# Splitting the causal convolution of sequence 1 over three engines in a fused Mamba and transformer kernel

## The chip, the cores and the metric

The kernel runs on one core of one Trainium2 chip, in one launch. The metric is device time in microseconds (us) of that core. Three runs of the kernel before gave 946.91, 949.45 and 950.11 us; their median is 949.45 us. A core has five engines that matter here: TensorE (PE, matrix products), VectorE (DVE), ScalarE (ACT), GpSimd (POOL) and SyncE (SP, which only issues DMAs). Each works through its own queue in order, and they wait for one another through semaphores. SBUF is the working memory, with 128 partitions; PSUM is the smaller memory into which TensorE writes its products, cut into banks.

## The reference

Four blocks with residuals and layer norms, on two sequences of 512 tokens with 512 features each. Only the first block matters here, a Mamba layer with 1024 channels, 16 states per channel and a causal convolution of four taps:

```python
proj = hidden_states @ W_in.T
x, gate = (proj[..., :D_IN], proj[..., D_IN:])
xpad = jnp.pad(x, ((0, 0), (K - 1, 0), (0, 0)))
xc = conv_b
for j in range(K):                               # K = 4
    xc = xc + conv_w[:, j] * xpad[:, j:j + L, :]
x = jax.nn.silu(xc)
...
state = state * dA + (dt_t * u_t)[..., None] * B_t[:, None, :]   # along time
y = jnp.einsum('bdn,bn->bd', state, C_t)
```

After it come a gated FFN with 4-bit weights ("gptq"), a small attention and a mixture block.

## The kernel before, in words

**Layout.** Channels lie on the partitions, in 8 blocks of 128 (index c), and the 512 time steps along the free dimension. A tile is 128x512 float32. The two sequences are handled one after the other (b = 0, 1).

**The scan loop.** The heart of the first block is the loop at L1152: 128 steps s, for b, then c, then gi (8 pairs of states). Step s handles a 128x1024 tile: DVE multiplies `du` by B (`times_B`, L1092; one step ahead, so step s computes the product for s+1), DVE runs the recurrence (`scan`, L1096), POOL multiplies by C (`times_C`, L1102), and TensorE adds the tile into `y` with an identity matrix (`sums`, L1124; two steps behind). ACT writes the decay factors exp(dt A) into one of two PSUM tiles (`exps`, L1076); those for step s+2 can be written only when scan s has read its tile. Every eighth step also has a `du` product (L1090) and a product of the gate with `y` (`fin`, L1130).

**What is planned beside it.** All other work of the neighbourhood is woven into these steps by a planner written in Python. A counter of ticks runs at two per step: the odd tick 2s+1 comes ahead of `times_B(s+1)`, the even tick 2s+2 between `times_B(s+1)` and `scan(s)`; `exps(s+2)` and `times_C(s)` come after the scan. A job is a generator that gives out some instructions and yields the number of ticks until it goes on. Jobs run in the order in which they were spawned. Extra work on POOL asks `pool_turn` (L181) for a turn, and there is one turn per step; who finds it taken tries again at the next tick. TensorE's extra products come from one generator, `stream` (L1030), in a fixed order; each step has a budget of 3.5 us (`STEP`), a product counts 0.86 us (`MM`), and `until` (L797) holds the stream back until a named job is done. `pin` (L407) fixes the order of tracing on PE, ACT, DVE and POOL, so the planner's order is the order of the queues. SP is not pinned.

**The jobs that share the steps 18 to 42.** They are

- `proj_x` and `x_job` (L787, L772): for each block c of sequence 1, four products into a PSUM bank `px`; then ACT evicts the bank with the newest tap and the bias into `u1_c` (`evict_x`, L478); two ticks later DVE adds the three older taps, each one an instruction that reads `px` and `u1_c` (`conv`, L485); two ticks later ACT makes a sigmoid (two instructions, L780 and L781); two ticks later, with a turn, POOL multiplies it in (L784). The convolutions lie in the steps 19, 22, 24, 27, 30, 32, 34 and 38, on even ticks: after `times_B(s+1)` and ahead of `scan(s)` on DVE's queue.
- the words of the 4-bit weights (`GateUpWords.steps`, L276): a new one every three steps; DVE takes out a nibble (L235), ACT converts it (L293), POOL subtracts and multiplies (L297, L301, a turn each), SP stores it. `stream` waits for the last word ("words") before it goes on to the gates of sequence 1.
- `gate` (L759) and `gate_job`: four products, three ACT instructions, one POOL product with a turn.
- `ranks1` and `rows1` (L862, L873): small products from all eight `u1_c`, after the last of these (`until(("u1", 7), 3)`); their result feeds the B and C tiles of sequence 1, which `states` (L553) loads in the steps 56 to 63. Then `fc1_expert` (L952) and `out_tiles` (L978), the latter from step 66 on, when `fin` of block 7 of sequence 0 is out.

Scratch rows come from small pools: `jrow` (tag "j", three buffers) and `trow` (tag "t", two buffers, for the sigmoids). The framework sets all semaphores from the accesses that it records. `ranks_out` (L542) is one more place that the prediction uses: there ACT (L544) and, for sequence 0, DVE (L548) copy two different parts of one PSUM tile `pt` to two different SBUF tiles.

Of the kernel before, what the change touches and what calls it, by code (L numbers as in the profile page):

```python
# [12 lines left out]
AF = mybir.ActivationFunctionType  # L13
# [7 lines left out]
S = 512  # L21
# [7 lines left out]
NCH = D_IN // P  # L29
# [4 lines left out]
KCONV = 4  # L34
# [22 lines left out]
def tile_sandwich(  # L57
# [5 lines left out]
    nc = tc.nc  # L63
# [34 lines left out]
    ch = const.tile([P, NCH, NCP], F32, name="ch")  # L98
# [82 lines left out]
    def pool_turn():  # L181

        while pool_at[0] == (now[0] - 1) // 2:
            yield 1
        pool_at[0] = (now[0] - 1) // 2
# [242 lines left out]
    with ExitStack() as mamba:  # L428
# [9 lines left out]
        def new_u(name):  # L438
            return up_.tile([P, S], F32, tag="u", name=name)
# [4 lines left out]
        def jrow(name):  # L444
            return jp.tile([P, S], F32, tag="j", name=name)

        def trow(name):
            return jp.tile([P, S], F32, tag="t", name=name, bufs=2)
# [7 lines left out]
        for b in range(B):  # L456
            t_ = smp.tile([R_DT + 1, S], F32, tag=f"dtT{b}", name=f"dtT{b}")
# [19 lines left out]
        def evict_x(c, ps, uc):  # L477
            nc.scalar.activation(  # L478
                uc, ps, AF.Identity,
                bias=ch[:, c, KCONV : KCONV + 1], scale=ch[:, c, KCONV - 1 : KCONV],  # L480
            )

        def conv(c, ps, uc):
            for s in range(1, KCONV):
                nc.vector.scalar_tensor_tensor(  # L485
                    uc[:, s:], ps[:, : S - s], ch[:, c, KCONV - 1 - s : KCONV - s],
                    uc[:, s:], ALU.mult, ALU.add,
                )
# [90 lines left out]
        with ExitStack() as p1:  # L579
# [5 lines left out]
            def bank1(i, name):  # L585
                return mbank(name) if i % 2 else ps_1.tile([P, S], F32, tag="mm", name=name)
# [28 lines left out]
            for c in range(NCH):  # L615
                w = w_in(0, 0, c)
                ps = bank1(c, f"px0_{c}")
                for k in range(KH):
                    nc.tensor.matmul(
                        ps, w[:, k, ts(c % 2, P)], xT[0][:, k, :], start=(k == 0), stop=(k == KH - 1)  # L620
                    )
                    if k == 1 and c >= 2:
                        for i in range(TB):
                            ranks_of(0, c - 2, i, pr)
                uc = u[0][c] = new_u(f"u0_{c}")
                evict_x(c, ps, uc)
                early = [gw.steps() for _ in range(4 if c == 0 else 0)]
                for word in early:
                    next(word)
                for word in early[:2]:  # L630
                    next(word)
                conv(c, ps, uc)
                nc.scalar.activation(uc, uc, AF.Silu)
                for word in early:
                    for _ in word:
                        pass
                if c:
                    gw.word()
                for _ in range((0, 0, 2, 0, 1, 0, 1, 0)[c]):
                    gw.word(nc.gpsimd)  # L640
# [42 lines left out]
        with ExitStack() as p2:  # L683
# [51 lines left out]
            def release(name):  # L735
                next(t for t in turns if t[0] == name)[1] = now[0]
# [35 lines left out]
            def x_job(c, ps):  # L772
                uc = u[1][c] = new_u(f"u1_{c}")
                evict_x(c, ps, uc)
                yield 2
                conv(c, ps, uc)
                release(f"px1_{c}")
                yield 2
                th = trow(f"tu1_{c}")
                nc.scalar.activation(th, uc, AF.Tanh, scale=0.5)  # L780
                nc.scalar.activation(th, th, AF.Identity, bias=half[:, 0:1], scale=0.5)  # L781
                yield 2
                yield from pool_turn()
                nc.gpsimd.tensor_mul(uc, th, uc)  # L784
                st["u1", c] = now[0]

            def proj_x(c):  # L787
                w = w_in(0, 1, c)
                if c + 2 - c % 2 < NCH:
                    w_in(0, 1, c + 2 - c % 2)  # L790
                while now[0] < 2 * (NGI * (c - 3) + 4):
                    yield None
                ps = yield from bank(f"px1_{c}")
                yield from in_proj(1, ps, w, c % 2)
                spawn(x_job(c, ps), 2)
# [402 lines left out]
        with ExitStack() as p3:  # L1198
# [9 lines left out]
            for j in range(NCH // 2):  # L1208
                w = wo_pair(1, 0, j)
                for e in range(2):  # L1210
                    c = 2 * j + e
# [305 lines left out]
```

## Time and profile before

| | |
|---|---|
| median of three runs | 949.45 us |
| the profiled execution | 943.15 us, its span 941.0 us |
| mean granted TensorE clock | 0.966 |
| busy: PE / DVE / ACT / POOL | 91% / 71% / 46% / 52% of the span |
| scan loop (first to last `times_C`) | 73.8 to 567.1 us |
| convolutions of sequence 1 | 141.0 to 226.1 us |

The profile is one execution recorded by the hardware. Its page has busy times by engine, a picture of the span in 40 slices, the chain of work that ended last, and groups of instructions by line. The trace behind it answers with timelines of one engine (start in us, duration in us, engine, line, operation, output<-inputs, shape, and in brackets the idle time ahead of it and who ended it), with waits, and with busy times in chosen windows. Consecutive instructions on an engine overlap by some hundredths of a microsecond, so three of 0.75 us in a row take 2.23 us. All times in the following are of this execution.

### The profile page before, as it was taken

What the parts mean: (1) busy time and instruction counts of PE and PEld (TensorE: products, weight loads), DVE (VectorE), ACT (ScalarE), POOL (GpSimd) and SP (SyncE); (2) the same over time, 40 slices, a digit from 0 to 9 for tenths busy, and PEclk for the clock granted to TensorE, in tenths of its full rate; (3) what the DMA queues carried; (4) which work ended last, traced back from release to release, by engine and by line L of the source; (5) the groups of instructions that cost most, each with busy time, mean ns of one, the idle gap of its engine ahead of it and who ended that gap; (6) DMA issues with size and microseconds to landing.
All of it is one profiled execution on the core that took longest, in us unless ns stands there. A gap on an engine that the chain in (4) does not pass through costs nothing.

```text
span 941.0 us, 7171 instructions
## 1 busy us (share of the span) xinstructions
PE 860.5 (91%) x2188; PEld 385.9 (41%) x2188; DVE 669.7 (71%) x770; ACT 428.3 (46%) x654; POOL 486.1 (52%) x356
## 2 busy tenths in 40 slices
PE   6989979879999898699999989899999998999994
PEld 3434433323544343244444434344544444445441
DVE  5778999999999998999999995525600034535235
ACT  3368875665667645656666530215320014322122
POOL 7758887767887777777788884520000000011012
PEclk9989999989999999799999999999999999999998
DMA  6549100110004954101110022356223121200101
GB/s 196 207 136 373 37 35 31 38 38 23 23 25 158 300 161 157 40 1 45 45 45 24 16 68 101 128 143 201 59 64 90 59 90 45 67 12 24 55 0 45
DMA packets 43816, 80.08 MB, mean 85 GB/s; under 512 B 7774, under 2 KB 20937, under 8 KB 43778
## 3 DMA queue, kind: packets, MB, share of 16 engines
q1 hardware_dynamic: 41506, 73.64, 24.0%
q0 software_dynamic: 1984, 5.47, 1.6%
q10 hardware_dynamic: 288, 0.52, 0.2%
q8 instruction: 17, 0.28, 0.1%
q14 instruction: 21, 0.17, 0.1%
HBM read 68.37 MB, written 11.24 MB: 85 GB/s over the span
## 4 chain that ended last, share of the span: by engine, by line
PE 40%; DVE 29%; issue 12%; DMA 5%; POOL 5%; ACT 3%; SPq 1%; DVEq 0%; POOLq 0%; ACTq 0%
DVE bx L1096 11%; DVE bx L1092 8%; PE pd L1445 6%; PE py L1124 5%; PE pup L1382 5%; PE fg L373 4%; PE fu L373 4%; PE fo L1298 3%; DMA B<-scr 2%; PE po L990 2%; DVE u L485 2%; PE fo L1235 2%; PE pr L1413 1%; POOL bx L1102 1%; PE pg L749 1%
## 5 line engine op out<-in xcount | busy, mean ns | idle before, releaser
L1102 POOL TENSOR_TENSOR bx<-bx,C 128x1024 f32<-128x1024 f32 x128 | 302.2, 2362 | 105.0 <-DVE bx L1096 77.9
L1096 DVE TENSOR_TENSOR_SCAN bx<-da,bx 128x1024 f32<-128x1024 f32 x128 | 291.7, 2279 | 0.3 <-ACT da L1076 0.2
L1124 PE MATMUL py<-bx,ident 128*128 128x512 f32 x480 | 234.5, 619 | 25.4 <-POOL bx L1102 21.8
L1076 ACT ACTIVATE da<-dt,A 128x511 f32<-128x511 f32 x256 | 176.5, 691 | 141.4 <-DVE bx L1096 136.8
L1092 DVE TENSOR_TENSOR bx<-du,B 128x1024 f32<-128x1024 f32 x127 | 152.9, 1205 | 3.8 <-POOL bx L1104 1.2
L1124 PEld LDWEIGHTS py<-bx,ident 128*128 128x128 f32 x480 | 91.9, 197 | 150.2 <-issue 97.3
L387 POOL TENSOR_TENSOR sd<-ve,half 128x4 f16<-128x4 f16 x2 | 2.1, 1042 | 113.1 <-DVE ve L385 113.1
L1311 DVE TENSOR_TENSOR it<-it,fu 128x512 f32<-128x512 f32 (+1 forms) x11 | 7.6, 687 | 73.6 <-PE fu L373 73.6
L749 PE MATMUL pg<-xT,w_g 128*128 128x512 f32 x114 | 56.3, 624 | 0.7 <-ACT dt L573 0.7
L1382 PE MATMUL pup<-hT_l,wup 128*128 128x512 f32 x128 | 56.2, 593 | 0.0
L1445 PE MATMUL pd<-wdn,hid 128*128 128x512 f32 x128 | 55.3, 593 | 0.0
L129 POOL TENSOR_TENSOR rs_lo<-ve_lo,mhalf 128x1 f32<-128x1 f32 x8 | 5.4, 680 | 76.7 <-DVE ve_lo L127 76.7
L1235 PE MATMUL fo<-wd,it 128*128 128x512 f32 (+1 forms) x88 | 40.0, 616 | 3.6 <-DMA wd<-wd_d 3.6
L1021 PE MATMUL fg<-hT_f,wg 128*128 128x512 f32 (+1 forms) x88 | 42.5, 594 | 0.0
L373 PE MATMUL fg<-hT_f,wg 128*128 128x512 f32 (+1 forms) x88 | 41.9, 615 | 0.7 <-ACT hT_f L173 0.7
L485 DVE SCALAR_TENSOR_TENSOR u<-px,ch,u 128x511 f32<-128x511 f32 (+2 forms) x48 | 35.9, 747 | 8.3 <-ACT u L478 7.1
L1021 PE MATMUL fu<-hT_f,wu 128*128 128x512 f32 (+1 forms) x88 | 40.4, 594 | 1.4 <-ACT dt L573 1.4
L373 PE MATMUL fu<-hT_f,wu 128*128 128x512 f32 (+1 forms) x88 | 39.8, 593 | 0.0
L1298 PE MATMUL fo<-wd,it 128*128 128x512 f32 (+1 forms) x88 | 39.6, 592 | 0.0
L1445 PEld LDWEIGHTS pd<-wdn,hid 128*128 128x128 f32 x128 | 24.2, 190 | 30.7 <-issue 30.1
L1310 ACT ACTIVATE it<-fg 128x512 f32<-128x512 f32 (+1 forms) x11 | 6.6, 597 | 65.7 <-PE fg L373 65.7
L1382 PEld LDWEIGHTS pup<-hT_l,wup 128*128 128x128 f32 x128 | 23.9, 190 | 28.2 <-issue 28.2
(243 smaller groups left out, 1168.2 us busy)
## 6 DMA issues: line engine op xcount, KB each, us to landing
wo<-in_W_outT SPq DMA_DIRECT2D x20, 512.0 KB
B<-scr SPq DMA_DIRECT2D x16, 512.0 KB
C<-scr SPq DMA_DIRECT2D x16, 512.0 KB
wg<-wgu_d SPq DMA_DIRECT2D x10, 512.0 KB
wu<-wgu_d SPq DMA_DIRECT2D x10, 512.0 KB
w_x<-in_W_in SPq DMA_DIRECT2D x8, 512.0 KB
wgu_d<-w_gu POOLq DMA_DIRECT2D x16, 256.0 KB, 2.4
w_g<-in_W_in SPq DMA_DIRECT2D x8, 512.0 KB
```

The source lines that it names most:

```text
L373: nc.tensor.matmul(ps[:m], w[:, kc, e * P : e * P + m], hT[:, kc, :], start=(kc == 0), stop=(kc == KH - 1),)
L749: nc.tensor.matmul(ps, w[:, k, ts(e, P)], xT[b][:, k, :], start=(k == 0), stop=(k == KH - 1))
L1021: nc.tensor.matmul(ps[:m], wt[j][a][:, kc, e * P : e * P + m], hT[:, kc, :], start=(kc == 0), stop=(kc == KH - 1),)
L1076: nc.scalar.activation(das[s % 2][:, i, 1:], st["dt", b, c][:, 1:], AF.Exp, scale=A[:, c, n : n + 1])
L1092: nc.vector.tensor_mul(bx, st["du"].unsqueeze(1).to_broadcast([P, NG, S]), Bbs[b][gi])
L1096: nc.vector.tensor_tensor_scan(flat, das[s % 2].rearrange("p n t -> p (n t)"), flat, 0.0, ALU.mult, ALU.add)
L1102: nc.gpsimd.tensor_mul(bxs[s], bxs[s], Cbs[b][s % NGI])
L1124: nc.tensor.matmul(st["y"], ident, bx[:, i, :], start=False, stop=last)
L1235: nc.tensor.matmul(fo[t], its[i][:m, ts(t, P)], w[:m, e], start=(i == 0), stop=(i == len(IC) - 1),)
L1298: nc.tensor.matmul(fo[t], its[i][:m, ts(t, P)], w[:m], start=(i == 0), stop=(i == len(IC) - 1),)
L1382: nc.tensor.matmul(ps, w[:, kc, ts(e, P)], src[kc], start=(kc == 0), stop=(kc == KH - 1))
L1445: nc.tensor.matmul(pd, hid[kc][:, ts(i, P)], wdn[kc], start=(kc == 0), stop=(kc == INT // P - 1),)
```

## The change

In the blocks c = 0 to 5 of sequence 1, the oldest of the four taps is taken from DVE. ACT scales the same PSUM bank by the oldest weight into a scratch row `ux1_c` (one tick after the eviction, one ahead of the convolution); DVE adds the other two older taps as before, and the bank is released at the same tick as before; POOL then adds the scratch row to `u1_c`, when it gets a turn. The sigmoid follows two ticks after that addition, and not two ticks after the convolution. The blocks 6 and 7 stay as they were, and so does sequence 0.

```diff
+        def tap(c, ps, t_):
+            s = KCONV - 1
+            nc.scalar.activation(t_[:, s:], ps[:, : S - s], AF.Copy, scale=ch[:, c, 0:1])
+
-        def conv(c, ps, uc):
-            for s in range(1, KCONV):
+        def conv(c, ps, uc, taps=KCONV):
+            for s in range(1, taps):
                 nc.vector.scalar_tensor_tensor(
                     uc[:, s:], ps[:, : S - s], ch[:, c, KCONV - 1 - s : KCONV - s],
                     uc[:, s:], ALU.mult, ALU.add,
...
             def x_job(c, ps):
                 uc = u[1][c] = new_u(f"u1_{c}")
                 evict_x(c, ps, uc)
-                yield 2
-                conv(c, ps, uc)
-                release(f"px1_{c}")
+                if c < NCH - 2:
+                    yield 1
+                    old = jrow(f"ux1_{c}")
+                    tap(c, ps, old)
+                    yield 1
+                    conv(c, ps, uc, KCONV - 1)
+                    release(f"px1_{c}")
+                    yield from pool_turn()
+                    nc.gpsimd.tensor_add(uc[:, KCONV - 1 :], uc[:, KCONV - 1 :], old[:, KCONV - 1 :])
+                else:
+                    yield 2
+                    conv(c, ps, uc)
+                    release(f"px1_{c}")
                 yield 2
                 th = trow(f"tu1_{c}")
                 nc.scalar.activation(th, uc, AF.Tanh, scale=0.5)
```

## The prediction

> **What bounds the kernel now.** I read the chain of waits first: between 145 and 239 us it runs almost wholly through DVE (scans, products with B, convolutions), then through TensorE to about 283 us, then through both in turn. Busy times in two windows say the same (columns: window, length, then busy us of PE, PE loads, DVE, ACT, POOL, each with its count; clock, DMA share, GB/s).
>
> ```profile
> 145.00:240.00 95.00, 79.88 (x169) 31.85 (x168) 93.77 (x77) 59.75 (x89) 71.10 (x42) 0.94 0.11 38
> 240.00:285.00 45.00, 45.00 (x151) 23.50 (x152) 43.75 (x30) 29.24 (x48) 37.32 (x22) 0.97 0.05 14
> ```
>
> From 145 to 240 us DVE has 1.2 us of idle time and everyone else has 15 or more; afterwards TensorE has none. So an instruction taken from DVE among the convolutions is worth its time, if nothing makes DVE wait instead. Next the timelines of DVE and of ACT around the convolution of block 3 (step 27); I read from them who is ready when.
>
> ```profile
> 175.25 1.22 DVE L1092 TENSOR_TENSOR bx<-du,B 128x1024 f32<-128x1024 f32 x1
> 176.38 2.31 DVE L485 SCALAR_TENSOR_TENSOR u<-px,ch,u 128x511 f32<-128x511 f32 x3
> ```
> ```profile
> 169.63 0.62 ACT L780 ACTIVATE tu<-u 128x512 f32<-128x512 f32 x1
> 170.29 0.72 ACT L781 ACTIVATE tu<-tu,half 128x512 f32<-128x512 f32 x1
> 171.03 1.28 ACT L573 ACT_TABLE_LOAD   x1
> 172.32 0.60 ACT L573 ACTIVATE dt<-pv 128x512 f32<-128x512 f32 x1
> 172.94 1.28 ACT L1076 ACT_TABLE_LOAD   x1
> 174.24 1.42 ACT L1076 ACTIVATE da<-dt,A 128x511 f32<-128x511 f32 x2
> 175.59 0.76 ACT L478 ACTIVATE u<-px,ch 128x512 f32<-128x512 f32 x1
> 176.25 1.41 ACT L1076 ACTIVATE da<-dt,A 128x511 f32<-128x511 f32 x2
> ```
>
> DVE begins the taps at 176.38, and at that moment ACT has just begun the decay factors of the next step. The new tap stands behind these in ACT's queue. That costs nothing unless DVE has to wait for it, and by the data it need not: tap and taps read the same bank and write different rows. Last, therefore, I looked for two engines that read one PSUM tile, in the timeline of all engines around 62 us.
>
> ```profile
> 62.41 0.57 ACT L544 COPY dtT<-pt 32x512 f32<-32x512 f32 x1 [1.58 <-PE pt L539]
> 63.01 0.68 DVE L548 COPY bc<-pt 32x512 f32<-32x512 f32 x1 [1.33 <-ACT dtT L544]
> ```
>
> Both copies only read `pt`, other partitions of it, and write different tiles. ACT starts when TensorE has finished; DVE does not, and is let go at 63.01, when ACT's copy ends (62.98). The reads are put one behind the other in the order of the program.
>
> **What goes.** Six DVE instructions. Three taps take 2.30 us as a row and 2.23 us up to the next instruction, so one is 0.743 us: 6 x 0.743 = 4.5 us off the bound. Block 6's wait of 0.34 us for its eviction goes too, since the sigmoids ahead of it on ACT move later. Together -4.8 us.
>
> **What comes on ACT, and the wait.** The tap is a Copy from PSUM with a scale per partition; the same form elsewhere (L1417, 128x512) takes 687 ns, about 0.65 us up to the next instruction. ACT has 35 us idle in the window, so 6 x 0.65 is hidden as work. As a wait it isn't, if the reads are serialized. The Trainium skill, in "PSUM — Partial Sum Buffer", section "PSUM bank collisions raise a hardware error", speaks against this change: two engines must not touch one bank and quadrant of 32 partitions at once, two reads included. By its quadrants the two copies of `pt` (partitions 0 to 31 and 32 to 63) could have run together; the row shows them apart, so here whole tiles are kept apart. By either, tap and taps (all 128 partitions) are. With the wait, DVE's second tap starts at the end of ACT's. Block by block, in the frame of the present trace (DVE ready; what ACT does before; tap's end):
>
> - c0: 141.03; decay factors to 141.6, a cast to 142.0; 142.65. Wait 1.6.
> - c1: 153.43; decay factors from 152.44, cast to 154.2; 154.85. Wait 1.4.
> - c2: 163.37; decay factors from 162.12 to 163.5; 164.15. Wait 0.8.
> - c3: 176.38. The sigmoids of blocks 1 and 2 (1.3 us each) now come later: one leaves its place ahead of the table load at 171.03, one enters ahead of the eviction, one ahead of the tap. 172.8 for the end of the table loads, +1.4 +1.3 +0.7 +1.35 +1.3 +0.65 = 179.5. Wait 3.1.
> - c4: 188.80; decay factors from 187.55; 189.4. Wait 0.6.
> - c5: 198.48; decay factors from 197.49 to 198.85, the sigmoid of block 3, tap; 200.85. Wait 2.4.
>
> The sum is 9.9 us. Behind the waiting tap on DVE stands `scan(s)`, and behind that `exps(s+2)`, `times_C` and TensorE's sums: all of it is late by the same amount. A delay of one block moves ACT's decay factors of the following steps too, so the waits add up. Bounds: 0, if the reads may overlap, and 9.9; I take 9.9, because the `pt` row is the same situation.
>
> **What comes on POOL.** Six additions of 128x509, each like L784 (1.27 us): 7.6 us, beside 24 us idle. In steps 25 to 28 an addition or a sigmoid product stands in every step, 2.31 + 1.23 us of POOL against 3.32 of DVE; POOL falls behind by at most 0.6 us and catches up at the next convolution. One price shows: a nibble on DVE that meets a busy POOL waits (2.22 us at 134.44 while L1102 runs, 0.32 otherwise). By my order the nibbles of steps 27 and 30 meet the last 0.1 and 0.3 us of such a product: 0.4 us; from 0 to 4 if the next L1102 goes first, but at 122.64 the nibble went in between (0.52 us), so 0.4. No DMA is added.
>
> So at step 42: -4.8 + 9.9 + 0.4 = **+5.5 us**.
>
> **What is moved.** Each addition takes a turn and delays a sigmoid, and both push the words. Block 0 evicts at tick 38, scales at 39, adds at 40, where the turn of step 19 is free. Block 1's taps are traced at tick 46, but the turn of step 22 has gone to block 0's sigmoid product and those of 23 and 24 to a word; it adds in step 25. Continued so, with earlier-spawned jobs first, the turns are: 19 add0, 20 and 21 word, 22 product of block 0, 23 and 24 word, 25 add1, 26 add2, 27 product 1, 28 product 2, 29 and 30 word, 31 add3, 32 word, 33 product 3, 34 word, 35 add4, 36 word, 37 product 4, 38 word, 39 add5, 40 product 6, 41 product 5, 42 product 7. (The same counting for the present kernel gives its POOL timeline.) The last word is through in step 38 in place of 34, block 7's product in 42 in place of 40. `stream` therefore starts the gates of sequence 1 in step 42 in place of 38, `ranks1` in 45 in place of 43, `rows1` in 56 in place of 52, and `fc1_expert` ends in 66, not 61. The eight gate products (6.9 us) leave a stretch where TensorE has room for one where it hasn't, but it idled in steps 50, 51 and 62 to 65, so they fit. In step 66 six products of `out_tiles` stood ahead of block 0's first sum; now three and two of `fc1_expert` do:
>
> ```profile
> 327.48 7.08 PE L990 MATMUL po<-wo,g 128*128 128x512 f32 x12 [1.31 <-DMA wo<-in_W_outT]
> ```
> ```profile
> 359.89 0.69 DVE L1130 TENSOR_TENSOR g<-g,py 128x512 f32<-128x512 f32 x1 [3.42 <-PE py L1124]
> ```
>
> Up to this `fin` (step 74) TensorE did 21 products of `out_tiles` and will do 16 (plus the two): three fewer net, at 0.92 us each 2.8 us, so most of the 3.42 us wait goes. Against it stand new waits of ACT for a gate, and of DVE for `y`, in steps 58 and 66, where TensorE is now full, some 1 to 2 us. By step 79 all output tiles are through in both orders. Net -1.7 us, between -3.4 (the whole wait) and +1. B and C of sequence 1 are written out four steps later, but B is used only seven steps after that; SP's word stores wait longer and delay no load that is due.
>
> **The sum.** 943.15 + 5.5 - 1.7 = 946.95 us for a profiled run. The median of the three runs is 6.3 us above that execution, so I carry over the difference: 949.45 + 3.8 = 953.2 us.
>
> **Rivals.** (1) The serialized read, as above: 953.2, chance 0.8 in all its sizes. It decides the sign from 4.8 us of waits on; the four blocks c0, c1, c3 and c5 alone hold 8.5. (2) The reads overlap, and the change does what it says: -4.8 + 0.4 - 1.7 = -6.1, so 943.3 us. For it: the addresses don't demand the wait. Against it: the `pt` row. Chance 0.13. (3) The late gates fill TensorE between 42 and 66 so far that it becomes the bound, +5.5 + 1 and no gain at `fin`: about 956. For it: 45.00 busy of 45.00. Against it: the idle steps. It is part of the 0.8. (4) POOL falls behind, and C holds up the sums: against it the 24 us idle; 0.07 with all else, such as nibbles that lose 2 us each.
>
> **Chances.** A measurement of this kernel tells about 0.3%, 2.8 us, from no change. Within the first case I give +1 to +8 us, so about a quarter lies below 2.8. Slower 0.61, same 0.21, faster 0.18. The range reaches from 945.5 to 957.5; it leaves out most of case 2 and the tail above +8, some 0.18 together.
>
> **What will show it.** Right: the first L485 of blocks 0 to 5 idle for 0.6 to 3.1 us with the new ACT line as releaser, 10 us in all; two L485 rows per block there; words' last product in step 38; the wait at the `fin` of step 74 mostly gone. Wrong: L485 starts while the tap is running. Then step 42 comes 4.4 us earlier, not later, and the rest of the sum is as in (2).

## The result and the profile after

The changed kernel takes 962.56 us (median of six runs, 955.41 to 967.47), against 948.65 us of the kernel before beside it (six runs). The ratio of the run times is 1.0133, with an interval of [1.0108, 1.0159]; of 948.65 us this is 12.6 us, between 10 and 15. (The ratio is not that of the two medians, which lie 13.9 us apart; differences given with an interval are worked out from ratios throughout.) The forecast was 953.2 us, slower by 3.8, with a range up to 957.5. The sign was right, and the time lies above the range. The profiled execution took 961.88 us (span 960.1, mean granted clock 0.955, before 0.966).

I lay the two traces side by side by the starts of the scans, one per step, from step 18 on (what lies ahead of that differed by 2.4 us in these two executions, what lies behind scan 126 by 5.9 us, and the change touches neither). Duration of each stage in us; the last two columns belong to experiments told further down.

| from scan to scan | before | after | difference | after, load asked for early | before with late gates, load asked for early |
|---|---|---|---|---|---|
| 18 to 42 (convolutions) | 103.01 | 108.14 | +5.1 | 108.51 | 103.02 |
| 42 to 55 | 47.87 | 45.94 | -1.9 | 47.80 | 47.93 |
| 55 to 65 | 34.62 | 35.52 | +0.9 | 35.51 | 35.50 |
| 65 to 66 | 3.91 | 10.42 | **+6.5** | 4.64 | 4.64 |
| 66 to 74 | 34.50 | 34.11 | -0.4 | 33.76 | 34.08 |
| 74 to 126 | 195.79 | 196.35 | +0.6 | 195.81 | 195.81 |

The first row is what I forecast (+5.5). The fourth is a loss in a single step that I did not have at all. First the convolutions. Timeline of DVE in the changed kernel, the two remaining taps of the blocks 0 to 5; in brackets the idle time ahead of the first one, and who ended it:

```profile
145.05 1.53 DVE L490 SCALAR_TENSOR_TENSOR u<-px,ch,u 128x511 f32<-128x511 f32 x2 [1.59 <-ACT ux L486]
...
158.13 1.53 DVE L490 SCALAR_TENSOR_TENSOR u<-px,ch,u 128x511 f32<-128x511 f32 x2 [1.35 <-ACT ux L486]
...
168.09 1.53 DVE L490 SCALAR_TENSOR_TENSOR u<-px,ch,u 128x511 f32<-128x511 f32 x2 [0.72 <-ACT ux L486]
...
183.49 1.53 DVE L490 SCALAR_TENSOR_TENSOR u<-px,ch,u 128x511 f32<-128x511 f32 x2 [3.09 <-ACT ux L486]
...
195.93 1.53 DVE L490 SCALAR_TENSOR_TENSOR u<-px,ch,u 128x511 f32<-128x511 f32 x2 [0.54 <-ACT ux L486]
...
207.16 1.53 DVE L490 SCALAR_TENSOR_TENSOR u<-px,ch,u 128x511 f32<-128x511 f32 x2 [2.24 <-ACT ux L486]
```

Each pair of taps waits for the tap on ACT, although it uses nothing that this writes. The six waits sum to 9.5 us; forecast were 1.6, 1.4, 0.8, 3.1, 0.6 and 2.4, together 9.9. Why block 3 waits longest is seen on ACT (timeline of the changed kernel, the answer to the one shown before):

```profile
176.89 1.41 ACT L1091 ACTIVATE da<-dt,A 128x511 f32<-128x511 f32 x2
178.24 0.61 ACT L795 ACTIVATE tu<-u 128x512 f32<-128x512 f32 x1
178.89 0.72 ACT L796 ACTIVATE tu<-tu,half 128x512 f32<-128x512 f32 x1
179.52 0.76 ACT L478 ACTIVATE u<-px,ch 128x512 f32<-128x512 f32 x1
180.18 1.40 ACT L1091 ACTIVATE da<-dt,A 128x511 f32<-128x511 f32 x2
181.52 0.61 ACT L795 ACTIVATE tu<-u 128x512 f32<-128x512 f32 x1
182.16 0.72 ACT L796 ACTIVATE tu<-tu,half 128x512 f32<-128x512 f32 x1
182.79 0.67 ACT L486 ACTIVATE ux<-px,ch 128x509 f32<-128x509 f32 x1
```

Two displaced sigmoids, an eviction and the decay factors of two steps stand ahead of a tap of 0.67 us, which ends at 183.46; DVE starts at 183.49. The busy times by window (columns as before) show the same stretch and the one behind it:

```profile
145.00:245.00 100.00, 78.78 (x157) 30.81 (x155) 91.26 (x72) 57.24 (x88) 73.43 (x44) 0.90 0.09 30
245.00:290.00 45.00, 45.00 (x152) 23.48 (x151) 44.74 (x31) 31.33 (x49) 36.22 (x20) 1.00 0.04 12
```

DVE, which bounds the first stretch, is now idle for 8.7 us of 100, where it was idle for 1.2 of 95. TensorE fills the second stretch as before. Now step 66. Timelines of POOL, SP, PE and DVE in the changed kernel around it:

```profile
325.49 2.35 POOL L1117 TENSOR_TENSOR bx<-bx,C 128x1024 f32<-128x1024 f32 x1 [0.23 <-DVE bx L1111]
```
```profile
327.87 0.32 SPq L565 DMA_DIRECT2D C<-scr  x1
328.28 0.38 SPq L113 DMA_DIRECT2D wex<-in_expert_w  x1
328.76 0.38 SPq L936 DMA_DIRECT2D wo<-in_W_outT  x1
```
```profile
327.21 1.88 PE L1139 MATMUL py<-bx,ident 128*128 128x512 f32 x4
332.94 3.05 PE L976 MATMUL pfe<-wex,wf1T 128*128 128x256 f32 x8 [3.85 <-DMA wex<-in_expert_w]
335.79 2.52 PE L1139 MATMUL py<-bx,ident 128*128 128x512 f32 x4
```
```profile
338.35 0.69 DVE L1145 TENSOR_TENSOR g<-g,py 128x512 f32<-128x512 f32 x1 [6.41 <-PE py L1139]
...
372.46 0.69 DVE L1145 TENSOR_TENSOR g<-g,py 128x512 f32<-128x512 f32 x1 [0.75 <-PE py L1139]
```

TensorE reaches the first products of `fc1_expert` at 329 us. Their weights `wex` were asked for at 328.28 and land 4.5 us later. Behind these products in TensorE's queue stand the sums of the last states of block 7, and DVE's `fin` (338.35) waits 6.41 us for them, and with DVE the scan. In the kernel before, the same load has long been there (timeline of SP):

```profile
288.71 0.34 SPq L560 DMA_DIRECT2D B<-scr  x1
289.99 0.33 SPq L113 DMA_DIRECT2D wex<-in_expert_w  x1
292.02 0.32 SPq L560 DMA_DIRECT2D B<-scr  x1
```

There it stands behind the first B of sequence 1, and is used at 307.68. In the changed kernel it stands behind the last C, that of the eighth pair of states (gi = 7). SP works in order, and this C leaves at 327.87 because POOL has to read the C of sequence 0 out of the same buffer first, in the product shown, which ends at 327.84. The other `fin` shown, that of step 74, waits 0.75 us where it waited 3.42: this gain was forecast.

The wait is not the whole loss. The eight products that follow it and the four sums take 5.37 us; in after_wex_traced_early, an experiment told below in which the load comes in time, the same twelve take 3.61 us. The granted clock differs (busy times by window, first the changed kernel, then that experiment):

```profile
332.94:338.31 5.37, 5.37 (x13) 3.26 (x13) 0.00 (x0) 0.00 (x0) 3.06 (x2) 0.68 0.09 34
329.34:332.95 3.61, 3.61 (x14) 2.17 (x12) 3.02 (x2) 2.70 (x4) 3.61 (x3) 1.00 0.82 229
```

At a clock of 0.68, 5.37 us hold the work of 3.65 us at full clock, so the clock accounts for the difference. Of the 6.5 us some 3.9 are the wait for the load, 1.8 the lower clock behind it, and 0.7 stay when neither is there (4.64 us against 3.91). That the clock is lower because TensorE has waited was not tested by itself. But in the five runs in which TensorE waits 2.6 us or more for `wex`, these eight products take 3.05 to 3.75 us, and in the four runs with late gates in which it waits 0.6 us or not at all, 1.89 to 1.97 us.

### The profile page after: what moved, and what is told of

It reads as the page before. It is cut to its first block, busy times and chain, and to the rows that moved or that the text cites. A ratio compares the mean times of both kernels' runs of the same rounds, so it can differ in the third digit from the quotient of the medians.

```text
span 960.1 us, 7185 instructions
## 1 busy us (share of the span) xinstructions
PE 868.7 (90%) x2188; PEld 390.1 (41%) x2188; DVE 666.6 (69%) x764; ACT 432.2 (45%) x660; POOL 493.1 (51%) x362
## 4 chain that ended last, share of the span: by engine, by line
PE 49%; DVE 22%; issue 8%; POOL 7%; ACT 5%; DMA 2%; SPq 1%; POOLq 0%; DVEq 0%; ACTq 0%
PE py L1139 9%; DVE bx L1111 9%; PE pd L1460 6%; DVE bx L1107 5%; PE pup L1397 5%; PE fu L373 4%; PE fg L373 4%; POOL bx L1117 3%; PE fo L1313 3%; PE fu L1036 3%; PE fg L1036 2%; PE pg L754 2%; PE fo L1250 2%; ACT da L1091 2%; PE pr L1428 1%
## 5 line engine op out<-in xcount | busy, mean ns | idle before, releaser
L1139 PE MATMUL py<-bx,ident 128*128 128x512 f32 x480 | 238.1, 627 | 30.8 <-POOL bx L1117 26.1
L373 PE MATMUL fu<-hT_f,wu 128*128 128x512 f32 (+1 forms) x88 | 42.2, 622 | 0.0
L490 DVE SCALAR_TENSOR_TENSOR u<-px,ch,u 128x511 f32<-128x511 f32 (+2 forms) x42 | 31.4, 748 | 15.5 <-ACT ux L486 9.5
L1036 PE MATMUL fu<-hT_f,wu 128*128 128x512 f32 (+1 forms) x88 | 40.5, 592 | 0.0
L754 PEld LDWEIGHTS pg<-xT,w_g 128*128 128x128 f32 x114 | 22.4, 201 | 33.0 <-issue 28.5
```

Source lines behind the costliest of these rows:

```text
L373: nc.tensor.matmul(ps[:m], w[:, kc, e * P : e * P + m], hT[:, kc, :], start=(kc == 0), stop=(kc == KH - 1),)
L754: nc.tensor.matmul(ps, w[:, k, ts(e, P)], xT[b][:, k, :], start=(k == 0), stop=(k == KH - 1))
L1036: nc.tensor.matmul(ps[:m], wt[j][a][:, kc, e * P : e * P + m], hT[:, kc, :], start=(kc == 0), stop=(kc == KH - 1),)
L1139: nc.tensor.matmul(st["y"], ident, bx[:, i, :], start=False, stop=last)
```

## The experiments

My theories after the result: (A) DVE's taps wait for ACT's tap because both read one PSUM tile, and the sum of the waits is what the change costs to step 42; (B) the loss at step 66 comes from the place of one load in SP's queue, which the late turns have moved. Rivals: (A') the taps wait for ACT's queue or for the written row, whatever it reads; (B') the late gates as such overfill TensorE. Twelve kernels were run, in three groups, each with the kernel before on the same chip. "Shift" is the start of a scan minus that of the kernel before, both counted from scan 18, in the one profile of each.

| run | median us | ratio | shift at 42 | at 65 | at 66 | at 126 |
|---|---|---|---|---|---|---|
| the change | 962.56 | 1.0133 [1.0108, 1.0159] | +5.1 | +4.1 | +10.6 | +10.8 |
| tap_from_sbuf | 948.69 | 0.9998 [0.9973, 1.0022] | -5.0 | -2.0 | +5.7 | +3.5 |
| add_without_turn | 951.40 | 1.0025 [1.0011, 1.0040] | +3.7 | +3.7 | +3.7 | +4.6 |
| late_gates | 954.50 | 1.0071 [1.0046, 1.0097] | 0.0 | +2.9 | +11.7 | +11.7 |
| wex_on_act | 953.07 | 1.0074 [1.0046, 1.0101] | +5.1 | +4.1 | +5.7 | +3.9 |
| extra_read | 955.07 | 1.0067 [1.0049, 1.0085] | +8.3 | +8.4 | +8.4 | +7.8 |
| late_gates_wex_on_act | 949.39 | 0.9995 [0.9974, 1.0016] | 0.0 | +2.8 | +8.1 | +7.9 |
| tap_early_no_turn | 943.20 | 0.9945 [0.9915, 0.9975] | -4.1 | -4.1 | -4.1 | -4.1 |
| tap_early_wex_on_act | 947.64 | 0.9970 [0.9948, 0.9992] | -4.3 | -1.6 | +3.9 | +1.4 |
| after_wex_traced_early | 952.57 | 1.0036 [1.0020, 1.0053] | +5.5 | +6.3 | +7.1 | +6.3 |
| late_gates_wex_traced_early | 947.85 | 0.9980 [0.9963, 0.9996] | 0.0 | +1.0 | +1.7 | +1.3 |
| tap_early_wex_traced_early | 944.24 | 0.9941 [0.9919, 0.9964] | -4.3 | -3.6 | -2.8 | -3.4 |
| two_taps | 942.92 | 0.9933 [0.9908, 0.9957] | -4.7 | -4.7 | -4.7 | -4.7 |

**The wait: the same tap from another memory.**

```diff
-                    tap(c, ps, old)
+                    tap(c, xs(1)[0], old)
```

> The changed kernel, but ACT's new instruction reads a row of x in SBUF and not the PSUM bank; place, size, addition and all turns stay (the oldest tap of six blocks is therefore wrong). Serialized reads of one PSUM tile (my theory): the six waits of DVE ahead of the two taps (9.5 us in the changed kernel) vanish, step 42 of the scan comes about 4.4 us earlier than in the kernel before, and everything after step 65 stays as slow as in the changed kernel, so about 9.5 us less than that: 951 to 954 us. Rival, the waits come from ACT's queue or the addition and have nothing to do with PSUM: the waits stay, 960 to 963 us.

The waits are gone. Timeline of DVE, block 3:

```profile
176.03 1.52 DVE L490 SCALAR_TENSOR_TENSOR u<-px,ch,u 128x511 f32<-128x511 f32 x2
```

The tap has its place, its length and the row that it writes, and only its source is another; DVE no longer waits, and step 42 comes 5.0 us early instead of 5.1 late. That excludes A'. The time, 948.7, came out some 2 us below the range that I had expected, although the loss at step 66 is there (+7.8 in this profile).

**The wait by itself: a read that nobody needs.** In the kernel before, where DVE keeps its three taps:

```diff
-                yield 2
+                yield 1
+                if c < NCH - 2:
+                    old = jrow(f"ux1_{c}")
+                    nc.scalar.activation(
+                        old[:, KCONV - 1 :], ps[:, : S - KCONV + 1], AF.Copy, scale=ch[:, c, 0:1]
+                    )
+                yield 1
                 conv(c, ps, uc)
```

> The kernel before with one thing added: in the six blocks ACT reads the bank into a scratch row one tick ahead of the convolution; nobody uses the row, DVE keeps its three taps and no turn moves. Theory of the serialized read: DVE waits for ACT by 1.6, 1.4, 0.8, 1.9, 0.6 and 1.0 us, 7.3 in all, step 42 is that much later, TensorE's idle time gives back about 2: 952 to 956 us. Rival, two reads don't exclude each other: no wait of DVE, 948 to 950 us.

```profile
157.54 2.32 DVE L485 SCALAR_TENSOR_TENSOR u<-px,ch,u 128x511 f32<-128x511 f32 x3 [2.20 <-ACT ux L778]
...
183.22 2.32 DVE L485 SCALAR_TENSOR_TENSOR u<-px,ch,u 128x511 f32<-128x511 f32 x3 [1.82 <-ACT ux L778]
```

The six waits are 1.35, 2.20, 0.71, 1.82, 0.72 and 0.97, together 7.8 us; the shift at step 42 is 8.3, stays so to step 66 and is 7.8 at step 126, and the time grows by 6.4 us [4.7, 8.1]. An unused read of a bank, 0.67 us of ACT, costs the bound 1.3 us per block on average (0.7 to 2.2).

**What goes, alone.**

```diff
-        def conv(c, ps, uc):
-            for s in range(1, KCONV):
+        def conv(c, ps, uc, seq1=False):
+            for s in range(1, KCONV - int(seq1 and c < NCH - 2)):
...
-                conv(c, ps, uc)
+                conv(c, ps, uc, True)
```

> The kernel before, with the oldest tap of the six blocks simply left out: what goes from DVE, and nothing in its place. By my sum -4.8 us at step 42 (six taps and the 0.34 us of block 6) and no other order anywhere, so 943.5 to 946. If it is no faster than the version with the early tap, the tap on ACT and the addition on POOL cost nothing by themselves, and the wait was their whole price.

The shift is -4.68 us at step 42 (the sum said -4.8) and stays so to step 126. The time is 6.4 us shorter [4.1, 8.7].

**The turns.**

```diff
-                    yield from pool_turn()
                     nc.gpsimd.tensor_add(uc[:, KCONV - 1 :], uc[:, KCONV - 1 :], old[:, KCONV - 1 :])
```

> The changed kernel, but POOL's addition is given out at once behind the two taps and takes no turn, so words, sigmoids, gates and the expert's weights keep the steps of the kernel before. My theory in two parts (waits for the PSUM read, then a weight load queued too late): DVE's six waits stay, step 42 comes 5.1 us later than before, but the wait of 6.4 us at the fin of step 66 is gone: 953 to 955 us. Rival, the later loss is caused by the delay itself and not by the turns: 960 us or more. A third, POOL with two extra products in a step becomes late: waits of TensorE for POOL grow and the time is above 956.

The sigmoids keep their places, so less stands ahead of the taps on ACT: the waits sum to 7.8 us, not 9.5. From step 42 to 66 the shift does not move, because the gates and the load are where they were. The time was below what was expected, for the first of these reasons.

**Late gates alone.** In the kernel before, `stream` waits eight ticks longer:

```diff
-                yield from until("words", 2)
+                yield from until("words", 10)
```

> The kernel before with one number changed: the gates of sequence 1 wait 10 ticks after the last word in place of 2, which puts them in step 42 as in the changed kernel; the convolutions are untouched. My theory: nothing changes up to step 42, then the expert's weight load stands behind the last C load on SP and DVE waits some 6 us at the fin of step 66; about 6 to 8 us slower than before, 954 to 957 us. Rival, the late gates alone are absorbed by TensorE's idle steps as I had predicted: 947 to 949 us.

Nothing of the convolution is changed, and the loss at step 66 is there. SP has the same order as in the changed kernel, and PE waits even longer:

```profile
331.64 3.64 PE L961 MATMUL pfe<-wex,wf1T 128*128 128x256 f32 x8 [6.22 <-DMA wex<-in_expert_w]
```

So step 66 belongs to the delayed gates. It doesn't tell yet whether by the load (B) or by TensorE's products (B').

**The load on another queue.** In the changed kernel, in the one with late gates alone, and in one with the early tap that follows:

```diff
-                ex = w4(expert_w, "wex", LAT // P, LAT)
+                ex = wst.tile([P, KH, PW], F32, tag="w4", name="wex")
+                nc.scalar.dma_start(out=ex[:, : LAT // P, :LAT], in_=expert_w)
```

> The changed kernel, but the load of the expert's weights is issued from ACT's queue and not from SP's, where it stood behind the last load of C. My theory: the wait of TensorE for it (3.85 us) and most of the 6.4 us wait of DVE at step 66 go; the waits for the PSUM read stay: 955 to 958 us. Rival, the load is slow because of the transfers beside it, from any queue: no change against the changed kernel, 960 to 963 us.

> The kernel before with the gates of sequence 1 in step 42 in place of 38, as in the run with late gates, and the expert's load from ACT's queue. Theory: of the 11.7 us by which the scan loop was later there, the 8.9 us at step 66 shrink to about 2: 948 to 951 us. Rival, the late gates cost by themselves: 953 us or more.

In the first, step 66 lost 1.6 us in place of 6.5, as B has it, and the time fell from 962.6 to 953.1. In the second the time came as expected, but the profile didn't: it still lost 5.3 us at step 66. The timeline of PE says why:

```profile
328.04 3.65 PE L962 MATMUL pfe<-wex,wf1T 128*128 128x256 f32 x8 [2.62 <-DMA wex<-in_expert_w]
```

The load left at 322.49, only 2.9 us before TensorE came to these products (325.42), and took 5.4 us; behind the wait the eight products take 3.65 us, not 1.89. ACT's queue is in order too, and there the load stands where `fc1_expert` is traced, between the decay factors of two late steps: it had left SP's queue, but went only 2.1 us earlier than in late_gates (324.62). This experiment had not removed the cause cleanly, and B' was still alive.

**The load asked for earlier.** It stays on SP, but the planner asks for it at the gate of block 6, two gates ahead:

```diff
                 for c in range(NCH - 4, NCH):
+                    if c == NCH - 2:
+                        ahead["f"] = w4(fc1_wT.rearrange("p k (a n) -> p (k a) n", n=PW), "wf1T")
+                        ahead["x"] = w4(expert_w, "wex", LAT // P, LAT)
                     yield from gate(1, c)
...
             def fc1_expert():
-                fT = w4(fc1_wT.rearrange("p k (a n) -> p (k a) n", n=PW), "wf1T")
-                fT = fT.rearrange("p (k a) n -> p k (a n)", k=LAT // P)
-                ex = w4(expert_w, "wex", LAT // P, LAT)
+                fT = ahead["f"].rearrange("p (k a) n -> p k (a n)", k=LAT // P)
+                ex = ahead["x"]
```

> The changed kernel, with the two loads of fc1_expert asked for at the gate of block 6 instead of after that of block 7. SP then has the load of the expert weights behind the C of block 3 and not behind that of block 7; its slot is free from about 316 us. If the place in SP's queue made the loss of 6.5 us at step 66, the load leaves at 316 to 319 us, TensorE no longer waits for it (3.85 us before), step 66 loses at most 2 us, and the time is 951 to 956. If the late gates themselves make that loss by filling TensorE, the step still loses 5 us or more and the time stays at 960 or above.

> The kernel before with the gates of sequence 1 as late as in the changed one, and the two loads asked for at the gate of block 6. On ACT's queue the load still left only 5.5 us ahead of its use, and the profile lost 5.3 us at step 66. Here it should leave near 315 us. If that load is all, step 66 loses at most 2 us in the profile and the time is 946 to 950, that of the kernel before. If late gates cost by themselves, 952 or more.

Timelines of SP, PE and DVE in after_wex_traced_early, and last the same `fin` on DVE in late_gates_wex_traced_early:

```profile
314.35 0.32 SPq L565 DMA_DIRECT2D C<-scr  x1
315.80 0.33 SPq L113 DMA_DIRECT2D wex<-in_expert_w  x1
```
```profile
329.34 1.89 PE L977 MATMUL pfe<-wex,wf1T 128*128 128x256 f32 x8
```
```profile
332.98 0.69 DVE L1149 TENSOR_TENSOR g<-g,py 128x512 f32<-128x512 f32 x1 [0.62 <-PE py L1143]
```
```profile
327.04 0.69 DVE L1134 TENSOR_TENSOR g<-g,py 128x512 f32<-128x512 f32 x1 [0.62 <-PE py L1128]
```

The load now stands behind the C of the fourth pair of states (the expectation says "block" for these pairs). It leaves 13.5 us ahead of its use, as soon as the gate products have set its buffer free (SP waits 1.1 us for them). In the changed kernel these products run 0.4 us earlier, so there the buffer had been free for some 12 us when the load left: it was not the buffer that held it. PE has no wait, `fin` waits 0.62 us instead of 6.41, and step 66 takes 4.64 us instead of 10.42 with every product of the late gates in place (fifth column of the stage table). The time is 952.57 us, 3.4 above the kernel before [1.9, 5.0]. With late gates alone, step 66 takes 4.64 us as well (sixth column), and the time is no longer than that of the kernel before: 0.998 [0.9963, 0.9996]. That is B, and B' falls.

**A version that beats both.** ACT scales the tap in the tick of the eviction, right behind it, so that the tap is over before DVE asks for the bank:

```diff
-                    yield 1
                     old = jrow(f"ux1_{c}")
                     tap(c, ps, old)
-                    yield 1
+                    yield 2
                     conv(c, ps, uc, KCONV - 1)
```

Once without the turn of the addition, so that no gate is late; once with turns, and the load on ACT; once with turns, and the load asked for earlier.

> The changed kernel with ACT's tap directly behind the eviction (a step earlier in ACT's queue, ahead of the decay factors) and POOL's addition without a turn. My theory: DVE finds the bank free, the six waits shrink to under 1 us together, step 42 comes 4.5 us earlier than before, and the expert's load is back at its old place: 943 to 946 us, faster than both kernels. Rival, the saving is lost later because TensorE becomes the bound from step 42 on: 947 to 950 us.

> The changed kernel with ACT's tap directly behind the eviction and the expert's load from ACT's queue; the additions keep their turns, so the gates are late. Theory: both causes are mended, step 42 comes 4.5 us earlier than before, step 66 has no wait for the expert's weights, and what is left is the shifted loads of the output weights (1 to 4 us): 945 to 949 us. Rival, something else in the late gates costs: above 950 us.

> The change with both of its side effects taken away and its turns kept: ACT scales the oldest tap in the tick of the eviction, and the two loads are asked for at the gate of block 6. No wait of DVE for that tap above 0.5 us (about -4.3 us at step 42) and a loss of at most 2 us at step 66: 942 to 946, as the version without turns (943.2). If turns and late gates cost something else, 947 or more.

In the first, one wait is left among the six blocks (timeline of DVE, block 3):

```profile
174.56 1.53 DVE L490 SCALAR_TENSOR_TENSOR u<-px,ch,u 128x511 f32<-128x511 f32 x2 [0.49 <-ACT ux L486]
```

It takes 943.20 us, 0.9945 [0.9915, 0.9975] of the kernel before, and the third takes 944.24, 0.9941 [0.9919, 0.9964]; they can't be told from each other, nor from two_taps, which does without the oldest tap altogether. The second gave 947.6: it has the remainder of the loss at step 66 (PE waits 3.1 us for the load). So with the tap in its right place, ACT's and POOL's work on it is free within what these runs can tell (some 3 us), as the change meant it to be.

## Why the forecast was right in its sign and wrong in its size

- **What goes** (-4.8): two_taps measured -4.68 us. Right.
- **What comes on ACT, and the wait** (+9.9): 9.5 us in the changed kernel, block by block within 0.2 us of the forecast; 0 when the tap reads other data, 7.8 when a read is added and nothing else. Right, and rival (2), reads that overlap, is excluded: in no run did ACT's and DVE's reads of `px` overlap. By its own sum, though, the prediction's sign turns at 6.1 us of waits and not at 4.8, since +0.4 and -1.7 count too. What the runs show is a wait for the whole tile (the two copies of `pt` read separate partitions), set by semaphores; the Trainium skill ("PSUM — Partial Sum Buffer", section "PSUM bank collisions raise a hardware error") says that the hardware would not stall two engines on one bank and quadrant but raise an error. Since the reads never met, this case shows the price of the rule and not its reason.
- **What comes on POOL** (+0.4): one nibble, that of step 30, took 0.50 us in place of 0.32; the others kept their length, so the term was 0.2. The three terms together gave +5.5 for step 42; measured +5.1. The list of turns held: the last word's product is in step 38, block 7's product in step 42, the gates from step 42 on. Rival (4) did not come.
- **What is moved** (-1.7): this step failed. I placed the gates' products, `fc1_expert` and `out_tiles` on TensorE anew, correctly, and closed with "so they fit" and with SP's word stores that "delay no load that is due". I asked what SP's stores would do to loads, and not which loads the moved steps themselves issue. `fc1_expert` is a moved step, it begins with two loads, and one of them came behind sixteen others in an in-order queue. Step 66 lost 6.5 us in the profile, 5.8 of which go when the load comes in time. By the ratios the load's place costs 12.6 less 3.4 us (962.56 and 952.57 us, each beside its own kernel before), some 9 us. A term for what a wait does to the granted clock was missing too. A single look at where `wex` stood in the order of SP (289.99, between the first B of sequence 1 and the second) would have put the question.
- The rest of that step had the right mechanisms. The wait at the `fin` of step 74 went from 3.42 to 0.75 us. The new waits came too, chiefly at the second load of `out_tiles`, which needs a buffer that `fc1_expert` now holds until 342 us: 2.27 us of PE in place of 1.31. Without the misplaced load the stages from step 42 on sum to +0.8 us (after_wex_traced_early) and +1.3 (late_gates_wex_traced_early), at the upper end of my -3.4 to +1 and just above it; the ratio of the latter puts them at -1.9 [-3.5, -0.4].
- **Rival (3)**, TensorE as the new bound, would have given 956, a time nearer to the measured one, for a cause that wasn't there. In the two runs with the load asked for early the wait at the `fin` of step 74 is 0.75 us, where it expected no gain, and late gates alone cost no time (0.998). Its size behind step 42, +1, is not excluded by the two profiles (+0.8 and +1.3).

With the load in place the changed kernel takes 952.57 us, 3.4 [1.9, 5.0] above its kernel before. The forecast of 953.2, 3.8 above, was a forecast of that kernel. That it comes so near is in part luck: in the profile of after_wex_traced_early the scan loop is 6.3 us late, +5.5 up to step 42 as forecast and +0.8 behind it in place of -1.7.

**What stays open.** One profile and the ratios of the run times differ by some us in the size of single terms. late_gates shifts the loop by 11.7 us in its profile, but the ratio gives 6.7 [4.4, 9.2]; late_gates_wex_on_act shows 7.9 and -0.5 [-2.5, +1.5]. The stretch behind scan 126, which no run touches, took between 382.3 us (granted clock 0.98) and 389.5 us (0.96) in these profiles, and the profiled execution of before lies 6 us below the median of its first three runs. For late_gates the profiled execution, 959.18 us, was near the slowest of its seven (952.18 to 959.27). And the stage from 42 to 55, 1.9 us shorter in the changed kernel, is not so in after_wex_traced_early, which does the same things in the same order there. Here too the clock differs: in the 21 us ahead of scan 42 it is 0.92 in the first and 0.84 in the second, and TensorE gets through 32 and 27 matrix instructions, so that in the second more is left to do behind scan 42. So the mechanism at step 66 is shown by the rows of the changed kernel, of late_gates and of the two kernels with the early load, and by these two kernels' times; its mean size, 6.5 us in one profile and 9 by the ratios, stays open within some 3 us.

## What to carry to other kernels

Before work is given to an idle engine, ask for each operand who else reads that tile and when: an instruction of 0.67 us cost the bound up to 3.1 us, because the engine that reads next had to wait for its place in the idle engine's queue; moved to the tick in which the tile had just been written, the same instruction was free. And where an edit delays a planned step, follow the loads that this step issues to their new place in their queue: ask what stands ahead of them there, and what those are waiting for. A load that had left 17.7 us ahead of its use became a wait of 6.4 us on the bound without a byte being added (3.9 us of it TensorE's wait for the load, most of the rest its slower products behind that wait), and moving the load to another in-order queue at the same point of the program cured it only in part, while asking for it two gates sooner left TensorE no wait.

## What the runs showed of the hardware that I had not expected

The load of `wex`, 256 KB, took 4.5 us in the changed kernel, 5.4 us in late_gates_wex_on_act and 6.9 us in late_gates, so a lead fitted to the first would have been too short in the others. And each wait of TensorE for `wex` of 2.6 us or more was followed by slower products: in late_gates, after 6.22 us of waiting, the eight products of 1.89 us took 3.64 us, and the twelve up to the `fin` ran at a granted clock of 0.68, as in the changed kernel after 3.85 us.
